# Moving scatters, key tiles, first maxima and row clears in a two-layer cross-attention and expert kernel

## The chip, the cores and the metric

The kernel runs on one core of a Trainium2 chip. The metric is the device time of one execution in microseconds (us). All data are 32-bit floats.

## The reference, cut to what matters

There are four batches of 512 rows of 256 numbers (`x`) and four contexts of 1601 rows. Two layers follow each other, and each is a cross-attention and then a mixture of experts:

```python
x = x + _L0_xattn_ref(ctx_1024, _layernorm(x), ...)   # 8 heads of 128, biases
x = x + _L0_ffn_ref(_layernorm(x), ...)               # 8 experts, top 2, capacity 512
x = x + _L1_xattn_ref(ctx_1024, _layernorm(x), ...)   # 8 heads of 32
x = x + _L1_ffn_ref(_layernorm(x), ...)               # 8 experts, top 2, no capacity
```

In the first expert layer each row goes to its two best experts. The rows of an expert are numbered in order of arrival, and each expert takes 512 of them:

```python
slot = jnp.where(valid, bin_ids * capacity + offsets, E * capacity)
xb = jnp.zeros((E * capacity + 1, hs), x.dtype).at[slot].set(xf[src])
h = jax.nn.gelu(jnp.einsum('ech,ehf->ecf', xb, w1))
y = jnp.einsum('ecf,efh->ech', h, w2).reshape(E * capacity, hs)
out = jnp.zeros((T, hs), x.dtype).at[src].add(flat_w[order][:, None] * yv)
```

The second attention is softmax(q k) v for each head, with keys and values projected from the raw context.

## The kernel before, in words

The kernel has four stages, one after the other.

Stage a, to 1609 us, is the first attention, batch after batch. While batch b is attended, the rows of batch b-1 are normalised, routed and scattered: `route` returns three steps. `normalize` is the layer norm, `choose` finds the two experts of every row and its slot, and `send` writes the rows with eight indirect DMAs from GpSimd's queue into a tensor in device memory, `slot_x` (L308). The scatters of one batch write the same tensor, so each waits for the one before. The last batch has no attention behind it, so its three steps lie in stage b.

Stage b is the first expert layer. Each expert's 512 slots are taken in two halves of 256: all eight experts run over half 0, then, after a branch, all eight over half 1. `all_experts` drives a half. For each expert `fetched` loads its rows from `slot_x` (sx, L1171) and its two weights (L1174, L1175), `turned` transposes the rows (L1183, L1184), `hidden` makes the hidden layer (L1193) with a Gelu (L1200), and `results` makes the output (L1207) and stores it into `slot_y` (L1216). Weights, rows and hidden tiles have two buffers. The first half holds only rows of the first three batches; the branch (L1282) reads whether that was so, and redoes the experts if not.

Beside the experts a generator does other work, two slices per expert: `keys_first` in half 0 (routing of the last batch, and the second attention's keys and values of batch 0, in 15 steps) and `keys_next` in half 1 (keys and values of batch 1, adding batch 0's expert outputs, batch 0's queries, and the score maxima of the attention's first unit). `collect` gathers expert outputs from `slot_y` with indirect DMAs on GpSimd's queue (L327); `add_collected` adds them to x on VectorE (L344).

A second generator, `clears`, writes constants into device memory with DMAs on SyncE's queue (SP), four per expert: the second halves of `slot_y` (eight of 256 KB), then `rows_a` and `rows_b` (41 of 530 KB, one of them half of that), which the last stage's scatters need in a cleared state. Their source is the tile `empty`. `tc.keep_in_program_order` holds a DMA behind what was written before it on its queue, and nothing more. Otherwise the order within a queue in this stage is drawn up by a scheduler that takes what is ready, earliest written first; so work can be drawn forward, across the branch too.

Stage c is the second attention, 16 units of (batch, group of four heads, half of the queries), each of 13 steps of one key tile. `maxima` makes the scores of a unit in seven pieces (L1109) and reduces them on VectorE (L1120). `negated` (L1129) and `to_row` (L1142, L1146) put the negated maxima into a row of the query tile `asked`. `weights` (L1357) multiplies `keyed`, which holds 32 key rows and a row of ones per head, with `asked`, and an Exp (L1370) makes the softmax weights. `add_weights` (L1379) sums them and `weigh` (L1388) multiplies them with the values. There are two `keyed` tiles, one for each group of heads; both are set to ones and zeros at the head of the stage (L1334, L1335) and filled by `load_keys` (L1341). The order of PE, VectorE, ScalarE and GpSimd is fixed as written in the steps. `put(step, f)` hangs work on a step; SP's order is left to the scheduler.

Stage d, from 2618 us, is the second expert layer. The pools `soon` and `turns` live from stage b to the end of stage c; the pools `b_...` and `c_...` live in their own stage, and a stage's pool takes over space of the stage before.

Of the kernel before, what the change touches and what calls it, by code (L numbers as in the profile page):

```python
# [8 lines left out]
F32 = mybir.dt.float32  # L9
I32 = mybir.dt.int32  # L10
AF = mybir.ActivationFunctionType
ALU = mybir.AluOpType
# [4 lines left out]
P = 128  # L17
B, S, D = 4, 512, 256
M = 1601
NT = S // P  # L20
NX = B * NT
DC = D // P
# [14 lines left out]
H1, DH1 = 8, 32  # L37
HG = P // DH1

E, FF = 8, 1024  # L40
# [4 lines left out]
CT = HALF // P  # L45
NOWHERE = 65536.0
# [11 lines left out]
PAY = D + 1 + E  # L58
# [12 lines left out]
def xattn_ffn_twice(ctx: ExitStack, tc: tile.TileContext, a: dict, out: bass.AP):  # L71
    nc = tc.nc
# [105 lines left out]
    slot_y = dram.tile([SLOTS, D], F32, name="slot_y")  # L178
# [160 lines left out]
    def add_collected(b, got, tiles=range(NT)):  # L339
        for t in tiles:  # L340
            for k in range(2):
                j = b * NT + t
                xs = x[b][:, t, :]
                nc.vector.scalar_tensor_tensor(  # L344
                    xs, got[2 * t + k], prob[k][:, j : j + 1], xs, ALU.mult, ALU.add
                )
# [31 lines left out]
        nc.sync.dma_start(rbias, a["br"].partition_broadcast(P))  # L378
        nc.sync.dma_start(b2, a["b2"])

    def clear_rows(empty):

        for rows in (rows_a, rows_b):
            n = rows.shape[0]
            for i in range(0, n, 4 * P):
                some = rows[i : min(i + 4 * P, n), :]

                tc.keep_in_program_order(
                    nc.sync.dma_start(
                        some.rearrange("(p r) d -> p r d", p=P),  # L390
                        empty.unsqueeze(1).to_broadcast([P, some.shape[0] // P, PAY]),
                    )
                )
                yield

    def route2(b, two, psum, tag, first=0, n=NT):

# [148 lines left out]
    with ExitStack() as st:  # L546
# [3 lines left out]
        rt = st.enter_context(tc.tile_pool(name="a_rt", bufs=1, side="right"))  # L550
        one = st.enter_context(tc.tile_pool(name="a_one", bufs=1))
# [333 lines left out]
        empty = scrap[:, 0, :]  # L885
# [14 lines left out]
        for n in range(n_steps + 4):  # L900
            b, h, t = n // (H0 * NT), n // NT % H0, n % NT
            if n < n_steps:
                if t == 0:
# [3 lines left out]
                    g = n // NT + 1  # L907
# [141 lines left out]
    for t in shift + asked:  # L1049
        nc.vector.memset(t, 0.0)  # L1050

    def queries(b, qT):
        xn = soon.tile([P, NT, D], F32, tag="xn", name="xn")
        mv = ln_moments(turns, x[b], NT)
        root = ln_root(turns, mv, NT)
        yield
        mv, rs = ln_scale(turns, mv, NT, root)
        for i in range(NT):
            ln_apply(xn, x[b], mv, rs, i)
        yield  # L1060
        xnT = soon.tile([P, DC, S], F32, tag="xnT", name="xnT")
        transposed(banks["s"], "s", xnT, xn, NT)
        yield
        for o in range(DC):
# [10 lines left out]
            yield  # L1075

    units = [(b, o, f) for b in range(B) for o in range(DC) for f in range(2)]
    qTs = {}

# [76 lines left out]
    with ExitStack() as st:  # L1156
# [8 lines left out]
        def slots(of, e, half):  # L1165
            s0 = e * CAP + half * HALF
            return of[s0 : s0 + HALF, :].rearrange("(t p) d -> p t d", p=P)

        def fetched(e, half):
            sx = two.tile([P, CT, D], F32, tag="sx", name="sx")  # L1170
            nc.sync.dma_start(sx, slots(slot_x, e, half))  # L1171
            w1 = two.tile([P, DC, FF], F32, tag="w1", name="w1")
            w2 = two.tile([P, FC, D], F32, tag="w2", name="w2")
            nc.sync.dma_start(w1, a["w1"][e].rearrange("(c p) f -> p c f", p=P))  # L1174
            nc.sync.dma_start(w2, a["w2"][e].rearrange("(c p) d -> p c d", p=P))  # L1175
            return e, half, sx, w1, w2

        def turned(e, half, sx, w1, w2):
            sxT = two.tile([P, DC, HALF], F32, tag="xT", name="sxT")
            tp = ps_t.tile([P, DC, CT, P], F32, tag="m", name="tp_x")  # L1180
            for c in range(DC):
                for t in range(CT):
                    nc.tensor.transpose(tp[:, c, t, :], sx[:, t, c * P : (c + 1) * P], ident)  # L1183
            nc.vector.tensor_copy(sxT, tp.rearrange("p c t q -> p c (t q)"))  # L1184
            return e, half, sxT, w1, w2
# [50 lines left out]
        empty = rt.tile([P, PAY], F32, name="empty")  # L1236
        nc.gpsimd.memset(empty, 0.0)
        nc.gpsimd.memset(empty[:, D : D + 1], NOWHERE)

        def clears():  # L1240

            for e in range(E):
                tc.keep_in_program_order(
                    nc.sync.dma_start(
                        slots(slot_y, e, 1), empty[:, :D].unsqueeze(1).to_broadcast([P, CT, D])
                    )
                )
                yield
            yield from clear_rows(empty)

        clear = clears()
        kvs = []

        def keys_first():
            normalize()
            yield
            choose()
            send()
            yield
            *kv, steps = keys_values(ps_s, "s", 0)  # L1260
            kvs.append(kv)
            for k, f in enumerate(steps):
                f()
                if k % 2:
                    yield

        normalize, choose, send = route(B - 1, rt, soon, ps_t, "m")
        all_experts(0, keys_first())
# [22 lines left out]
        def keys_next():  # L1291
            *kv, steps = keys_values(ps_s, "s", 1)
            kvs.append(kv)
            for f in steps[:6]:
                f()
            yield
# [12 lines left out]
            negated(0)  # L1309
            to_row(0)  # L1310

        all_experts(1, keys_next())
        assert next(clear, None) is None

# [5 lines left out]
    with ExitStack() as st:  # L1320
# [5 lines left out]
        ps_m = st.enter_context(tc.tile_pool(name="c_ps_m", bufs=1, space=PSUM))  # L1326
        banks.update(s=ps_s, m=ps_m)

        keyed = [one.tile([P, 2, M], F32, name=f"keyed{o}") for o in range(DC)]
        of_ones = ones[:, 0:1].to_broadcast([P, M])
        for t in keyed:
            nc.scalar.activation(t[:, 0], of_ones, AF.Copy, scale=in_row[:, 0:1])  # L1334
            nc.vector.tensor_scalar(t[:, 1], of_ones, in_row[:, 0:1], None, ALU.mult)  # L1335

        def load_keys(b, o):
            for pair in range(2):
                for s in range(2):
                    i = 2 * pair + s  # L1340
                    nc.sync.dma_start(  # L1341
                        keyed[o][64 * s : 64 * s + 32, pair, :],
                        kvs[b][0][o][i * DH1 : (i + 1) * DH1, :],
                    )


        by_pool = (1, 4, 7, 10)
# [121 lines left out]
        def put(step, *fs):  # L1469
            at.setdefault(step, []).extend(fs)  # L1470
# [9 lines left out]
        for b in range(B):  # L1480
# [20 lines left out]
            if 1 <= b and b + 1 < B:  # L1501
# [8 lines left out]

                spread(s0 + 2, projected(), 2, 16)
        put(per_batch * (B - 1) + 4, load_first_weights)

        load_keys(0, 0)
        load_keys(0, 1)
        ordered = st.enter_context(in_order(*computing))

        for g in range(3):
            maxima(1, g)
        ahead = {}  # L1520
        for u in range(1, n_units):
            for g in range(len(pieces)):
# [422 lines left out]
```

## Time and profile before

| what | value |
|---|---|
| median of three runs | 2953.87 us (2949.18 to 2956.38) |
| profiled execution | 2949.11 us |
| its span | 2947.0 us |
| PE busy | 2770.3 us (94%) |
| VectorE, ScalarE, GpSimd busy | 1466.2, 937.7, 392.5 us |
| mean granted TensorE clock | 0.973 |
| stage a, to 1590 us: PE busy | 1553.65 of 1590.0 us |
| stage b, 1590 to 1927 us: PE busy, DMA share | 308.70 of 337.0 us, 0.77 |
| stage c, 1927 to 2618 us: PE busy, DMA share | 602.62 of 691.0 us, 0.13 |
| stage d, 2618 to 2947 us: PE busy, DMA share | 305.29 of 329.0 us, 0.51 |

A line of busy time by stretch gives the stretch, its length, the busy time of each engine with its number of records, the granted clock (1.00 is full), the mean busy share of the 16 DMA engines, and GB/s. A matmul of this kernel shows as two records. A timeline line gives start, duration, engine, source line, operation, and in brackets the engine's idle time before it with what ended it. "SPq" is a queue's own instruction, such as the issue of a DMA.

### The profile page before, as it was taken

What the parts mean: (1) busy time and instruction counts of PE and PEld (TensorE: products, weight loads), DVE (VectorE), ACT (ScalarE), POOL (GpSimd) and SP (SyncE); (2) the same over time, 40 slices, a digit from 0 to 9 for tenths busy, and PEclk for the clock granted to TensorE, in tenths of its full rate; (3) what the DMA queues carried; (4) which work ended last, traced back from release to release, by engine and by line L of the source; (5) the groups of instructions that cost most, each with busy time, mean ns of one, the idle gap of its engine ahead of it and who ended that gap; (6) DMA issues with size and microseconds to landing.
All of it is one profiled execution on the core that took longest, in us unless ns stands there. A gap on an engine that the chain in (4) does not pass through costs nothing. (4 is left out here: it accounts for less than half of the span.)

```text
span 2947.0 us, 36216 instructions
## 1 busy us (share of the span) xinstructions
PE 2770.3 (94%) x13686; PEld 1883.4 (64%) x13686; DVE 1466.2 (50%) x2333; ACT 937.7 (32%) x1325; POOL 392.5 (13%) x301
## 2 busy tenths in 40 slices
PE   6999999999999999999999799988989898889997
PEld 2666667666766666666666587744444444467886
DVE  6445456544575544454444202267767768742110
ACT  3323334233342333332332112134434344331221
POOL 0000000100001000010000101021314233333442
PEclk9999999999999999999999899999999999999999
DMA  5444443343434333343346798610101021035663
GB/s 162 113 108 113 104 112 85 102 106 92 104 98 109 95 91 92 89 109 94 91 99 185 199 255 235 185 46 16 30 28 48 19 66 63 11 114 154 180 188 82
DMA packets 197448, 314.94 MB, mean 107 GB/s; under 512 B 44007, under 2 KB 118056, under 8 KB 194440
## 3 DMA queue, kind: packets, MB, share of 16 engines
q1 hardware_dynamic: 157512, 227.52, 29.1%
q0 software_dynamic: 15168, 49.23, 5.7%
q10 hardware_dynamic: 24576, 35.68, 4.7%
q8 instruction: 114, 1.87, 0.3%
q14 instruction: 78, 0.64, 0.1%
HBM read 114.64 MB, written 51.86 MB: 56 GB/s over the span
## 5 line engine op out<-in xcount | busy, mean ns | idle before, releaser
L806 DVE TENSOR_REDUCE top<-ps_s 128x1 f32<-128x2113 f32 x128 | 301.9, 2358 | 585.2 <-PE ps_s L798 585.2
L835 PE MATMUL ps_o<-pT,v 128*128 128x256 f32 x2176 | 521.1, 381 | 0.5 <-DVE inv L813 0.5
L798 PE MATMUL ps_s<-kT,qT 128*128 128x512 f32 (+1 forms) x1280 | 488.8, 526 | 6.5 <-ACT attn L812 6.4
L835 PEld LDWEIGHTS ps_o<-pT,v 128*128 128x128 f32 x2176 | 410.0, 191 | 114.5 <-issue 68.3
L812 ACT ACTIVATE attn<-ps_s,top 128x2113 f32<-128x2113 f32 x128 | 258.9, 2023 | 477.5 <-DVE top L806 433.2
L798 PEld LDWEIGHTS ps_s<-kT,qT 128*128 128x128 f32 x1280 | 241.8, 191 | 252.9 <-issue 236.5
L827 DVE STREAM_TRANSPOSE pT<-swapped 128x2176 f32<-128x2176 f32 x128 | 312.4, 2441 | 31.0 <-DMA swapped<-attn 20.4
L1120 DVE TENSOR_REDUCE tops<-ps_s 128x2 f32<-128x1024 f32 (+1 forms) x224 | 238.1, 1105 | 149.6 <-PE ps_s L1109 149.2
L747 PE MATMUL ps_k<-kvin,wkv 128*128 128x512 f32 (+1 forms) x640 | 263.8, 535 | 4.1 <-DVE mv_g L685 2.1
L1357 PE MATMUL ps_w<-asked,keyed 64*128 64x256 f32 (+1 forms) x1664 | 244.7, 416 | 21.1 <-DVE tops L1120 9.6
L781 PE MATMUL ps_v<-wkv,kvin 128*128 128x256 f32 x1088 | 254.6, 381 | 0.7 <-ACT v L788 0.6
L1357 PEld LDWEIGHTS ps_w<-asked,keyed 64*128 64x128 f32 (+1 forms) x1664 | 147.5, 190 | 146.6 <-ACT pT L1370 61.8
L1370 ACT ACTIVATE pT<-ps_w 128x1024 f32<-128x1024 f32 (+1 forms) x176 | 179.3, 1023 | 193.7 <-PE ps_w L1357 191.9
L781 PEld LDWEIGHTS ps_v<-wkv,kvin 128*128 128x128 f32 x1088 | 205.0, 190 | 35.9 <-ACT v L788 6.0
L1379 DVE TENSOR_TENSOR sum<-sum,pT 128x1024 f32<-128x1024 f32 (+1 forms) x128 | 183.2, 1431 | 10.4 <-ACT pT L1370 4.0
L760 ACT ACTIVATE kT<-ps_k,bqk 128x512 f32<-128x512 f32 (+1 forms) x160 | 96.8, 620 | 266.5 <-DMA swapped<-attn 129.0
L1379 POOL TENSOR_TENSOR sum<-sum,pT 128x1024 f32<-128x1024 f32 x48 | 122.6, 2554 | 347.5 <-ACT pT L1370 347.3
L747 PEld LDWEIGHTS ps_k<-kvin,wkv 128*128 128x128 f32 x640 | 116.4, 192 | 78.5 <-issue 67.4
L1109 PE MATMUL ps_s<-kv,qT 32*128 32x512 f32 (+1 forms) x1024 | 135.4, 574 | 14.6 <-ACT kv L1013 6.5
L788 ACT COPY v<-ps_v 128x512 f32<-128x512 f32 x144 | 79.7, 560 | 217.0 <-PE ps_v L781 150.2
L1193 PE MATMUL ps_h<-sxT,w 128*128 128x256 f32 x512 | 116.7, 386 | 2.9 <-ACT hT L1200 2.1
L1207 PE MATMUL ps_y<-w,hT 128*128 128x256 f32 x512 | 114.4, 380 | 0.2 <-DVE y L1215 0.2
(282 smaller groups left out, 2731.5 us busy)
## 6 DMA issues: line engine op xcount, KB each, us to landing
swapped<-attn SPq DMA_DIRECT2D x1536, 68.0 KB, 2.1
swapped<-attn ACTq DMA_DIRECT2D x512, 68.0 KB, 2.2
w<-in_w_dram SPq DMA_DIRECT2D x32, 1024.0 KB, 10.2
rows_b<-empty SPq DMA_DIRECT2D x36, 530.0 KB, 11.3
w_e<-in_wall_dram SPq DMA_DIRECT2D x4, 2052.0 KB, 9.3
cw<-in_ctxT_dram SPq DMA_DIRECT2D x4, 1601.0 KB, 12.5
keyed<-kv SPq DMA_DIRECT2D x32, 200.1 KB, 3.8
ctx_b<-in_ctx_dram SPq DMA_DIRECT2D x3, 1536.0 KB, 8.0
```

What stands on the lines that cost most here:

```text
L747: nc.tensor.matmul(ps[:, :n], lhsT=wkv[:, c, hs], rhs=kvin[:, c, : NB - 1, k, :] if k < 4 else kvin[:, c, NB - 1, :, :], start=c == 0, sto ...
L781: nc.tensor.matmul(ps[:, k, :], lhsT=flat_kvin[c][:, j * P : (j + 1) * P], rhs=wkv[:, c, cols], start=c == 0, stop=c == DC - 1,)
L798: nc.tensor.matmul(flat[:, j0 : j0 + n], lhsT=qT[:, t * P : (t + 1) * P], rhs=kT[:, j0 : j0 + n], start=True, stop=True,)
L806: nc.vector.tensor_reduce(top, flat[:, :L], AX.X, ALU.max, negate=True)
L812: nc.scalar.activation(attn[:, :L], flat[:, :L], AF.Exp, bias=top, accum_out=total)
L827: nc.vector.transpose(pT[:, :, k * P : (k + 1) * P].rearrange("p c (a i) -> p a c i", a=4), swapped.rearrange("p a (c i) -> p a c i", i=32),)
L835: nc.tensor.matmul(ps, lhsT=v[:, j - parts[part][0], (h % 2) * DH0 : (h % 2 + 1) * DH0], rhs=pT[:, j, :], start=j == 0, stop=j == NB - 1,)
L1109: nc.tensor.matmul(pss[i // 2][:, i % 2, at : at + n], lhsT=qTs[b][rows, o, q0 : q0 + P], rhs=kvs[b][0][o][rows, j0 : j0 + n], start=True, ...
L1120: nc.vector.tensor_reduce(tops[u][:, t : t + at // n, 2 * pair : 2 * pair + 2, j0 // 512], of, AX.X, ALU.max,)
L1357: nc.tensor.matmul(ps[:r, s, pair * QH : (pair + 1) * QH], lhsT=keyed[o][64 * s : 64 * s + 64, pair, j * P : j * P + r], rhs=asked[u % 3][ ...
L1370: nc.scalar.activation(pT[:r], ps[:r], AF.Exp)
L1379: (nc.gpsimd if k else nc.vector).tensor_tensor(to, to, pT[:r], ALU.add)
```

## The change

The change does six things:

1. `send()` of the last batch, written before between `choose` and the keys of batch 0, is written in the 21st slice of half 0, which lies after expert 7's rows are fetched.
2. `all_experts` gives the side work three slices per expert instead of two, and the key steps of half 0 come one per slice.
3. The first of the two key tiles moves into the pool `soon`. It is set in the 21st and loaded in the 22nd slice of half 0. The second stays in stage c; it is set in step 4 and loaded in step 8.
4. The first three maxima of unit 1, written before at the head of stage c, come after unit 0's in half 1, and `to_row(0)` comes after the first of them.
5. The row clears leave stage b. They are written one by one in steps 2 to 42 of stage c.
6. The clears of `slot_y` are written one per expert of half 0, and `empty` moves into `soon`.

```diff
-    def clear_rows(empty):
+    def clear_rows():
+        def clear(some):
+            tc.keep_in_program_order(
+                nc.sync.dma_start(
+                    some.rearrange("(p r) d -> p r d", p=P),
+                    empty.unsqueeze(1).to_broadcast([P, some.shape[0] // P, PAY]),
+                )
+            )
         for rows in (rows_a, rows_b):
             n = rows.shape[0]
             for i in range(0, n, 4 * P):
...
+                yield lambda some=rows[i : min(i + 4 * P, n), :]: clear(some)
...
+    keyed = [soon.tile([P, 2, M], F32, name="keyed0")]
...
+    def init_keys(t):
+        of_ones = ones[:, 0:1].to_broadcast([P, M])
+        nc.scalar.activation(t[:, 0], of_ones, AF.Copy, scale=in_row[:, 0:1])
+        nc.vector.tensor_scalar(t[:, 1], of_ones, in_row[:, 0:1], None, ALU.mult)
+    empty = soon.tile([P, PAY], F32, name="empty")
...
             for e in range(E):
                 done = hidden(*here)
                 next(beside, None)
-                for _ in range(4):
-                    next(clear, None)
+                if half == 0:
+                    clear_results(e)
                 if e + 1 < E:
                     here = turned(*fetched(e + 1, half))
+                next(beside, None)
                 if last:
                     results(*last)
                 next(beside, None)
...
             normalize()
             yield
             choose()
-            send()
             yield
             *kv, steps = keys_values(ps_s, "s", 0)
             kvs.append(kv)
-            for k, f in enumerate(steps):
+            for f in steps:
                 f()
-                if k % 2:
-                    yield
+                yield
+            for _ in range(len(steps) + 2, 3 * E - 4):
+                yield
+            send()
+            init_keys(keyed[0])
+            yield
+            load_keys(0, 0)
...
-            for f in steps[:6]:
-                f()
-            yield
-            add_collected(0, got0)
-            for k, f in enumerate(steps[6:]):
+            for k, f in enumerate(steps):
+                if k == 6:
+                    add_collected(0, got0)
                 f()
                 if k % 3 == 2:
                     yield
...
             negated(0)
-            to_row(0)
+            for g in range(3):
+                maxima(1, g)
+                yield
+                if g == 0:
+                    to_row(0)
...
-        keyed = [one.tile([P, 2, M], F32, name=f"keyed{o}") for o in range(DC)]
-        of_ones = ones[:, 0:1].to_broadcast([P, M])
-        for t in keyed:
-            nc.scalar.activation(t[:, 0], of_ones, AF.Copy, scale=in_row[:, 0:1])
-            nc.vector.tensor_scalar(t[:, 1], of_ones, in_row[:, 0:1], None, ALU.mult)
...
+        keyed.append(one.tile([P, 2, M], F32, name="keyed1"))
...
-        load_keys(0, 0)
-        load_keys(0, 1)
+        for k, f in enumerate(clear_rows()):
+            put(2 + k, f)
+        put(4, lambda: init_keys(keyed[1]))
+        put(8, lambda: load_keys(0, 1))
         ordered = st.enter_context(in_order(*computing))
-        for g in range(3):
-            maxima(1, g)
```

More of the change, by code (lines that the diff above doesn't have):

```diff
@@ L385, in clear_rows @@
             for i in range(0, n, 4 * P):
[L386 to L393, printed above, removed]
-                yield
+                yield lambda some=rows[i : min(i + 4 * P, n), :]: clear(some)
     def route2(b, two, psum, tag, first=0, n=NT):
@@ L1050, in xattn_ffn_twice, with load_keys @@
         nc.vector.memset(t, 0.0)
+    keyed = [soon.tile([P, 2, M], F32, name="keyed0")]
+    def load_keys(b, o):
+        for pair in range(2):
+            for s in range(2):
+                i = 2 * pair + s
+                nc.sync.dma_start(
+                    keyed[o][64 * s : 64 * s + 32, pair, :],
+                    kvs[b][0][o][i * DH1 : (i + 1) * DH1, :],
+                )
+    def init_keys(t):
[3 more added lines that the diff above has]
+    empty = soon.tile([P, PAY], F32, name="empty")
+    nc.gpsimd.memset(empty, 0.0)
+    nc.gpsimd.memset(empty[:, D : D + 1], NOWHERE)
     def queries(b, qT):
@@ L1075, in queries @@
             yield
+    kvs = []
     units = [(b, o, f) for b in range(B) for o in range(DC) for f in range(2)]
@@ L1234, in all_experts, with clear_results @@
             assert next(beside, None) is None
[L1236 to L1246, printed above, removed]
-                )
-                yield
-            yield from clear_rows(empty)
-        clear = clears()
-        kvs = []
+        def clear_results(e):
+            tc.keep_in_program_order(
+                nc.sync.dma_start(
+                    slots(slot_y, e, 1), empty[:, :D].unsqueeze(1).to_broadcast([P, CT, D])
+                )
+            )
         def keys_first():
@@ L1261, in keys_first @@
             kvs.append(kv)
-            for k, f in enumerate(steps):
+            for f in steps:
                 f()
-                if k % 2:
-                    yield
+                yield
[5 more added lines that the diff above has]
+            load_keys(0, 0)
         normalize, choose, send = route(B - 1, rt, soon, ps_t, "m")
@@ L1293, in keys_next @@
             kvs.append(kv)
-            for f in steps[:6]:
-                f()
-            yield
-            add_collected(0, got0)
-            for k, f in enumerate(steps[6:]):
+            for k, f in enumerate(steps):
+                if k == 6:
+                    add_collected(0, got0)
                 f()
@@ L1309, in keys_next @@
             negated(0)
-            to_row(0)
+            for g in range(3):
[3 more added lines that the diff above has]
+                    to_row(0)
         all_experts(1, keys_next())
-        assert next(clear, None) is None
     with ExitStack() as st:
@@ L1327, in xattn_ffn_twice @@
         banks.update(s=ps_s, m=ps_m)
-        keyed = [one.tile([P, 2, M], F32, name=f"keyed{o}") for o in range(DC)]
-        of_ones = ones[:, 0:1].to_broadcast([P, M])
-        for t in keyed:
-            nc.scalar.activation(t[:, 0], of_ones, AF.Copy, scale=in_row[:, 0:1])
[L1335 to L1344, printed above, removed]
+        keyed.append(one.tile([P, 2, M], F32, name="keyed1"))
         by_pool = (1, 4, 7, 10)
```

## The prediction

> **What bounds the kernel now.** I began with the slices of the page: PE is at 9 almost everywhere, with a 7 in the 23rd (1621 to 1695 us) and 8s from the 27th on (1915 us). As the change touches only the expert stage and the head of the attention, I next took busy time by stretch there, cut where the waits lie.
>
> ```profile
> core 0: us, PE busy (x) PEld busy (x) DVE busy (x) ACT busy (x) POOL busy (x), PEclk, DMA share, GB/s
> 1590.00:1657.20 67.20, 65.94 (x294) 51.33 (x292) 27.90 (x87) 15.04 (x24) 4.95 (x6) 1.00 0.81 238
> 1657.20:1677.90 20.70, 0.03 (x2) 0.01 (x1) 0.23 (x1) 1.54 (x2) 5.87 (x6) 0.59 0.27 74
> 1677.90:1690.00 12.10, 11.32 (x42) 9.27 (x43) 0.87 (x2) 2.08 (x4) 0.00 (x0) 0.72 0.94 278
> 1690.00:1769.00 79.00, 79.00 (x375) 69.05 (x374) 7.21 (x14) 12.25 (x21) 0.00 (x0) 1.00 1.01 251
> ...
> 1800.00:1926.70 126.70, 126.52 (x610) 101.87 (x610) 26.50 (x33) 19.85 (x35) 0.00 (x0) 1.00 0.66 184
> ```
>
> The reader is to see that PE is full in every stretch of this stage but the second, which is empty, and that the clock is 0.59 there and 0.72 after it. In 1690 to 1769 the DMA engines are full too (1.01), yet PE waits for none of it: the row clears ride along for nothing.
>
> The waits of PE, and those of SP's queue, give the empty stretch one cause; the timeline gives its course.
>
> ```profile
> PE tp_x L1183 <- DMA sx<-slot_x: 20.7, 1, 20.7
> ...
> SPq L1171 <- DMA slot_x<-xn,slot: 23.2, 1, 23.2
> ```
>
> ```profile
> 1638.07 0.99 POOL L308 DMA_INDIRECT slot_x<-xn,slot  x1 [15.03 <-ACT kv L112]
> 1649.64 0.98 POOL L308 DMA_INDIRECT slot_x<-xn,slot  x1 [10.58 <-DMA slot_x<-xn,slot]
> ...
> 1672.74 0.98 POOL L308 DMA_INDIRECT slot_x<-xn,slot  x1 [1.55 <-DMA slot_x<-xn,slot]
> 1675.12 0.89 SPq L1171 DMA_DIRECT2D sx<-slot_x  x2
> ...
> 1677.89 1.12 PE L1183 MATMUL tp_x<-ident,sx 128*128 128x128 f32 x4 [20.67 <-DMA sx<-slot_x]
> 1679.04 0.69 DVE L1184 COPY sxT<-tp_x 128x512 f32<-128x512 f32 x1 [21.56 <-PE tp_x L1183]
> 1679.79 6.11 PE L1193 MATMUL ps_h<-sxT,w 128*128 128x256 f32 x16 [0.78 <-DVE sxT L1184]
> ```
>
> Eight scatters go one at a time: each waits for the one before to land (11.6 us while the DMA engines are full, 2.6 us at the end). Expert 2's rows are read from the same tensor, so their load stands behind the eighth scatter. Everything else on PE, batch 0's keys included, has been drawn forward and is used up at 1657.2.
>
> Second place, the chain of waits where experts end and attention begins:
>
> ```profile
> 1927.81 2.14 DMA slot_y<-y
> 1930.36 0.88 issue
> 1931.23 1.05 DVE keyed L1335
> 1932.28 1.15 DVE tops L1120
> 1933.47 4.34 PE ps_s L1109 x12
> 1937.81 2.06 PE ps_w L1357 x8
> 1939.93 1.28 ACT L1370
> 1941.23 1.03 ACT sum L1370
> ```
>
> Experts end at 1927.0, and the first Exp starts at 1941.2: 14.2 us in which the output store has to land, the key tiles are set, and unit 1's maxima stand ahead of the first weights.
>
> **What the Trainium skill says.** "TensorE: Matmul & The Clock Gate", What's actually happening: PE's clock halves after an idle window of about 3.4 us and comes back after about as long at work. The trace agrees: 16 ps_h records take 6.11 us after the stall, 3.62 us otherwise. "DMA: Bandwidth & Descriptors", Anatomy of one DMA — SWDGE (gpsimd) path: about 2 us of a DMA are fixed, mostly the receipt of its last write. The trace's chained scatters at 2.6 us agree. The same page, Issuing engines are not separate DMA queues: DMAs of every engine share the same 16 engines. The 11.6 us of the second scatter, issued beside four clears, agrees.
>
> **Part by part.** *Scatters.* They are now written after expert 7's first-half load, and as writes to a tensor still being read they can't be drawn ahead of it. Expert 2's load then depends only on scatters of older batches, done by 1330 us. Gone: 20.7 us of waiting, 0.8 us for the copy after it, 2.5 us of slow ps_h and 0.5 us of slow tp_x: **24.5 us**. PE's next limit is its own work: 14.3 us an expert, beside which 2.5 MB an expert need 10 us at the 251 GB/s seen. What is late next is the scatters themselves. Expert 7's load is issued at 1711.7, the halves' last results end at 1769.0 and the next half's load goes at 1775.7: cover of 64 us less about 3 us of landing, so 61 us for eight, or 7.6 us each. The eight took 37 us in all before, the first two in the worst load; without clears the DMA share falls by about half, and batch 2's eight, at a share of 0.41 around 1315 us, were issued 2.7 to 3.8 us apart; I take 3 to 6 us each, 24 to 48 us. Cost 0, bounds 0 and 29 us (second rival). POOL has the gathers of batch 0 behind them; they start at the branch anyway.
>
> *Row clears.* 41 DMAs, 22 MB, leave the experts and go to SP's queue in attention steps 2 to 42. No PE time was lost to them, so none comes back, except at the start of half 1: four clears there hold SP for 11.2 us, and the gather on the chain takes 6.3 us to land. Of 5.4 us idle in 1769 to 1800, 3.3 are the branch's; I take **1 us**, bounds 0 and 2. In the attention 22 MB at 251 GB/s are 88 us; DMA share there is 0.1. Queued near them on SP: the query loads (written 12 steps ahead, 34 us at 2.8 us a step) and the second key load (steps 8 to 26, about 50 us); on POOL's queue the gathers, added 13 steps after issue. A clear's landing of 11.3 us fits each slack. Cost 0, bounds 0 and 5. SP draws ready DMAs ahead of their step, as it does now with the query loads (asked<-qT x8 at 1861, the last at 1870), so some seven clears will land among the last experts: 3.8 MB, 15 us, against a weight lead of 21 us (one and a half experts). That too costs 0.
>
> *Result clears.* Eight as before, one per expert. The zero row moves to a pool that opens only when the first attention has ended (SP's cw load waits there for x L856 until 1612), so the first goes at 1612 instead of 1593; results are read after the branch only. If SP stood at it, expert 1's weights behind it would come some 17 us late, of which expert 0's results on PE cover 7: cost 0, bounds 0 and 10.
>
> *Keys and maxima.* Three maxima of unit 1 go beside the half-1 experts: 3 x 1.07 us on PE, which is full there, so +3.2 us before the experts' end, and the row of unit 0 (0.6 us) with them; DVE's 6 reduces (6.9 us) lie under PE (DVE is busy 26 of 127 us). keyed0 is set and loaded in half 0. At the boundary remain y's copy and its store landing (1930.3, 3.3 us after the experts' end), since the attention's tiles lie where y was; ps_w (1.1 us) and the table load (1.28 us) fit in that, or 1.3 us stick out. Before 14.2 us, after 3.2 + 0.6 + 3.3 to 4.6: a gain of 5.8 to 7.1, I take **6.5 us**. keyed1 is set in step 4: DVE 1.05 us and ACT 1.62 us, written in order; DVE has no gap from 1955 to 1967, so I charge **1.3 us**, bounds 0 and 2.7. keyed0's ACT 1.62 us before a Gelu may hold PE once: **0.3 us**.
>
> *Three slots of side work per expert instead of two* reorder PE's work, not its sum. I charge **1 us** for PSUM turns of closely placed maxima (bounds -1 and 3).
>
> Sum: -24.5 - 1 - 6.5 + 1.3 + 0.3 + 1 = **-29.4 us**. The profiled execution took 2949.1 us (span 2947.0 and 2.1 around it); the sum gives 2919.7 for it. It was as fast as the fastest of the three runs, whose median is 2953.87; for a median I predict **2924 us**.
>
> **Rivals.** *Boundary gain lost*: the first Exp waits for something else (the table load, DVE's backlog of 1955 to 1967, a store behind clears), so only the stall is gained: -22 us, 2932. For it: DVE is the limit soon after. Against: 9 us of DVE work leave that place.
>
> *The stall moves to the half boundary*: under weights alone each scatter still takes the 11.6 us of the worst case; 93 us against 61 leave 32, some 3 of it filled by batch 1's keys: 29 us lost of 29, about 2953. For it: the first three took 11.6, 8.2 and 4.6 us. Against: clears were in the queue then. From 7.6 us per scatter PE waits.
>
> *Slower: the clears stand ahead of loads that the attention needs.* At the 2.8 us that SP took per clear at its worst (11.16 us for four), 41 are 114 us. If all of them stood ahead of the second key load, needed 26 steps or 75 us in, unit 2 would start 39 us late: 2963. It starts to wait from 27 clears ahead and ends slower from 38. For it: SP draws ready DMAs forward. Against: each clear is held behind what is already written on SP, and only seven are written before that load.
>
> *The change doesn't do what it says*: if the load stayed behind the scatters, only the boundary would gain: 2947. A read can't need a later write, so I hold this unlikely.
>
> **How the numbers follow.** Forecast 0.66 (2916 to 2933); boundary lost 0.15 (2930 to 2943); stall moved 0.08; not done 0.04; slower 0.07. A measurement of this kernel tells about 0.3%, 9 us, from no change, so faster means below 2945. Faster 0.83 (the first two and a rest), same 0.10 (the stall moved, or not done), slower 0.07. The range, 2912 to 2944, holds the forecast with its unknown costs and nearly all of the second case.
>
> **What would show it.** Right: no wait of tp_x for sx over 3 us; scatters between about 1685 and 1740 with the last landed before the branch; first half's results ending near 1744; the first Exp within 5 us of the last expert; clears spread on SP from the last experts to about 2030 and no wait of PE, DVE or ACT on keyed, asked or g. Wrong: a wait of SP's sx load on slot_x after the branch; a wait of ps_w on keyed; new PE gaps in the first half by DVE or ACT.

## The result and the profile after

Six runs of the changed kernel had a median of 2926.10 us (2920.64 to 2930.95), six of the kernel before, run beside it, 2953.22 us. The ratio is 0.9909, with a 95% interval of 0.9894 to 0.9923: 27 us faster. The profiled execution took 2930.95 us, the slowest of the six; its span is 2929.2 us.

Busy time by stretch, after. The first three cuts are those shown of before; the fourth ends with half 0's last result, the fifth with half 1's.

```profile
core 0: us, PE busy (x) PEld busy (x) DVE busy (x) ACT busy (x) POOL busy (x), PEclk, DMA share, GB/s
1590.00:1657.20 67.20, 66.39 (x311) 54.16 (x310) 30.09 (x88) 16.74 (x25) 3.39 (x6) 1.00 0.59 195
1657.20:1677.90 20.70, 20.70 (x99) 18.22 (x98) 2.08 (x3) 4.16 (x7) 0.00 (x0) 1.00 0.55 171
1677.90:1690.00 12.10, 12.10 (x56) 9.70 (x55) 1.11 (x2) 2.38 (x4) 0.99 (x1) 1.00 0.50 174
1690.00:1746.10 56.10, 56.10 (x259) 47.66 (x259) 5.44 (x12) 7.75 (x13) 6.85 (x7) 1.00 0.44 143
1746.10:1919.10 173.00, 161.89 (x735) 124.75 (x733) 45.26 (x72) 28.80 (x48) 8.18 (x8) 0.97 0.74 203
```

The second stretch, which held 0.03 us of work, is now full. PE is full to the end of half 0, and the DMA share there is 0.44 where it was 1.01. The last line is the surprise: half 1 takes 173 us with 11 us of idle PE.

Waits of PE from 1590 to 1922 us (total, times, longest): sx has left the list, and smaller waits stand in its place.

```profile
PE ps_h L1218 <- ACT hT L1225: 4.2, 2, 3.9
PE ps_k L1008 <- PEq L1304: 3.3, 1, 3.3
PE ps_s L1134 <- DVE tops L1145: 1.8, 3, 0.7
PE ps_w L1365 <- DVE y L1240: 0.8, 1, 0.8
PE ps_y L1232 <- DVE y L1240: 0.8, 1, 0.8
PE ps_h L1218 <- DMA w<-in_w_dram: 0.7, 1, 0.7
```

The timeline of GpSimd: the scatters lie beside half 0, 2.5 to 7.1 us apart, and the first gather behind the branch finds them long done.

```profile
1688.46 0.99 POOL L308 DMA_INDIRECT slot_x<-xn,slot  x1 [61.88 <-DMA sx<-slot_x]
1691.51 0.98 POOL L308 DMA_INDIRECT slot_x<-xn,slot  x1 [2.06 <-DMA slot_x<-xn,slot]
...
1717.01 0.98 POOL L308 DMA_INDIRECT slot_x<-xn,slot  x1 [6.07 <-DMA slot_x<-xn,slot]
1719.53 0.98 POOL L308 DMA_INDIRECT slot_x<-xn,slot  x1 [1.54 <-DMA slot_x<-xn,slot]
1750.53 1.05 POOL L327 DMA_INDIRECT g<-slot_y,slot  x1 [30.02 <-DVEq L1304]
```

The timeline at the boundary to the attention:

```profile
1917.84 1.24 PE L1232 MATMUL ps_y<-w,hT 128*128 128x256 f32 x5
1919.12 0.69 DVE L1240 COPY y<-ps_y 128x512 f32<-128x512 f32 x1 [7.27 <-PE ps_y L1232]
1919.86 1.13 PE L1365 MATMUL ps_w<-asked,keyed 64*128 64x256 f32 x8 [0.79 <-DVE y L1240]
1922.32 1.28 ACT L1378 ACT_TABLE_LOAD   x1 [17.47 <-PE ps_s L1134]
1923.61 2.03 ACT L1378 ACTIVATE sum<-ps_w 128x1024 f32<-128x1024 f32 x2
```

Experts end at 1919.08, and the first Exp starts 4.5 us later. PE's ps_w waits for y's copy alone (0.79 us), but it isn't what the Exp waits for last. ScalarE's sequencer, the part that issues its instructions, holds the table load until the store of the last y has landed: the store is issued at 1919.84 and lands at 1921.95, and the sequencer, waiting on that store's semaphore since 1904.26, goes on at 1921.98. (The timeline names ps_s, which ended at about the same time; in "spaced, clears later" the table load starts at 1911.06, after the store's landing at 1910.90 and before ps_s ends at 1911.16.) So y's copy, the landing of its store and the table load of 1.28 us make up the 4.5 us. Before, the key tiles and unit 1's maxima came on top.

A table by stretch, for all kernels run, carries the rest. *Half 0* goes from the start of stage a's last record of x (L856, now L858) to the end of half 0's last ps_y, *half 1* from there to the end of the last ps_y, the *boundary* from there to the first Exp, the *attention* from there to the last `got`. The ratio is to the kernel before, run beside it. The stretches of a row come from one profiled execution, the median from four to twenty. Executions of one kernel differ by some us in a stretch, as the two rows of before and of changed show, and the profile of "clears later" is the slowest of its four, 8 us above their median.

| kernel | half 0 | half 1 | boundary | attention | median us | ratio [95%] |
|---|---|---|---|---|---|---|
| before | 157.8 | 158.0 | 14.2 | 665.4 | 2953.22 | 1 |
| before, again | 160.7 | 163.3 | 14.2 | 665.7 | 2960.84 | 1.0000 [0.9992, 1.0007] |
| changed | 132.2 | 172.9 | 4.5 | 665.2 | 2926.10 | 0.9909 [0.9894, 0.9923] |
| changed, again | 132.9 | 172.2 | 4.5 | 659.8 | 2924.25 | 0.9903 [0.9886, 0.9920] |
| scatters late alone | 140.4 | 167.5 | 14.2 | 667.3 | 2940.56 | 0.9944 [0.9930, 0.9957] |
| scatters early again | 149.7 | 179.0 | 4.5 | 661.7 | 2945.53 | 0.9963 [0.9949, 0.9977] |
| clears back | 149.9 | 171.7 | 4.3 | 659.7 | 2936.92 | 0.9940 [0.9925, 0.9956] |
| edge back | 131.4 | 180.4 | 12.9 | 665.1 | 2945.09 | 0.9972 [0.9963, 0.9982] |
| edge back, clears later | 131.1 | 167.2 | 12.9 | 664.1 | 2928.01 | 0.9898 [0.9883, 0.9914] |
| maxima back | 132.2 | 176.3 | 9.2 | 660.8 | 2930.93 | 0.9922 [0.9905, 0.9938] |
| maxima back, clears later | 132.6 | 166.1 | 9.2 | 663.4 | 2923.20 | 0.9888 [0.9872, 0.9904] |
| clears later | 132.7 | 173.3 | 4.3 | 664.2 | 2922.87 | 0.9889 [0.9873, 0.9904] |
| spaced | 132.8 | 168.0 | 4.5 | 659.9 | 2921.91 | 0.9894 [0.9876, 0.9912] |
| spaced, clears later | 132.2 | 163.1 | 4.4 | 658.4 | 2916.10 | 0.9864 [0.9849, 0.9879] |

### The profile page after: what moved, and what is told of

Read it like the earlier page. It is cut to its first block, busy times and chain, and to the rows that moved or that the text cites. A ratio compares the mean times of both kernels' runs of the same rounds, so it can differ in the third digit from the quotient of the medians.

```text
span 2929.2 us, 36226 instructions
## 1 busy us (share of the span) xinstructions
PE 2773.5 (95%) x13686; PEld 1883.9 (64%) x13686; DVE 1464.3 (50%) x2333; ACT 936.2 (32%) x1324; POOL 393.4 (13%) x301
```

## The experiments

**The two kernels again.** The changed kernel, unchanged:

> The changed kernel itself, for a second profile and as the measure of the three beside it. Theory: stall of the scatters gone (half 0 about 25 us shorter), boundary 10 us shorter, half 1 about 9 to 15 us longer; the wait of 3.9 us for a Gelu at the start of half 1 hangs on when the gathers land and will differ between executions. Expected 27 us (0.9909) below the kernel before. Rival: all that was seen in the first profile belongs to the change, so half 1 is again 173 us and the time 18 to 20 us below.

It came out at 0.9903, so the gain stands; half 1 is again 172 us, as the rival had it. The kernel before, for a second profile of it:

> The kernel before, unchanged, for a second profile of it. The changed kernel's own two profiles differ by 5.4 us in the attention (665.2 and 659.8 us from the first Exp to the last unit's output); the one profile of before has 665.4. Theory (the attention takes one of two courses by chance, in either kernel): 659 to 667 us here, and half 0, half 1 and the boundary as in the first profile within 1 us (157.8, 158.0, 14.2). Rival (the changed order at the attention's head makes the shorter course likelier, and before always takes the longer one): 665 to 667 us, and 2952 to 2956 in all.

The attention took 665.7 us, which fits either expectation and settles nothing between them. "Half 1 as in the first profile within 1 us" failed: it took 163.3 us instead of 158.0. Its list of waits has the reason:

```profile
PE tp_x L1183 <- DMA sx<-slot_x: 22.0, 2, 21.6
PE ps_h L1193 <- ACT hT L1200: 6.0, 2, 5.7
```

ps_h's wait for the first Gelu is 5.7 us here and was 1.8 us in the profile that the prediction rested on. That is 4 of the 5 us. The stall is nearly the same in both (21.6 and 20.7 us).

**Scatters late alone.** The kernel before, with `send()` alone moved:

```diff
             choose()
-            send()
             yield
...
+            for _ in range(5):
+                yield
+            send()
```

> The kernel before, with the eight scatters of the last batch alone written later (behind expert 7's first-half load); clears, keys and maxima stay where they were before. Theory (the stall is gained by the scatters' place alone): half 0 takes 132 to 134 us from stage a's end instead of 158, half 1 and the boundary stay at 158 and 14 us; about 24 us faster than before, 2930. Rival (beside the clears, with the DMA engines full, each scatter takes up to 11.6 us, so eight take 93 us against a cover of 61): tp_x waits for sx some 30 us at the start of half 1, and the time stays at 2953 or rises.

0.9944: 16 us, two thirds of what the theory gave. Half 0 is 8 us longer than in the changed kernel. PE lost that to a late weight load, which SP issued at 1725.15 behind five clears (8.44 us), and to the slow matmuls behind the wait:

```profile
1742.43 9.24 PE L1207 MATMUL ps_y<-w,hT 128*128 128x256 f32 x32 [5.43 <-DMA w<-in_w_dram]
```

GpSimd's timeline shows the rival's slow scatters too, if at 6.2 to 10.9 us each instead of 11.6:

```profile
1695.92 0.99 POOL L308 DMA_INDIRECT slot_x<-xn,slot  x1 [72.86 <-ACT hT L1200]
1704.88 0.98 POOL L308 DMA_INDIRECT slot_x<-xn,slot  x1 [7.97 <-DMA slot_x<-xn,slot]
1715.79 0.98 POOL L308 DMA_INDIRECT slot_x<-xn,slot  x1 [9.93 <-DMA slot_x<-xn,slot]
...
1759.87 0.98 POOL L308 DMA_INDIRECT slot_x<-xn,slot  x1 [8.66 <-DMA slot_x<-xn,slot]
1763.43 1.05 POOL L327 DMA_INDIRECT g<-slot_y,slot  x1 [2.58 <-SPq L1285]
```

The eight take 64 us, and PE's wait at the branch, which ends after the last is issued, is 6.4 us instead of 3.3. The rival's wait of tp_x for sx did not come. By stretch:

```profile
1660.00:1690.00 30.00, 30.00 (x133) 23.92 (x132) 3.88 (x6) 5.35 (x9) 0.00 (x0) 1.00 1.04 211
1690.00:1751.70 61.70, 56.27 (x257) 48.67 (x256) 4.75 (x11) 7.17 (x12) 6.87 (x7) 0.94 1.08 258
```

The DMA share is 1.04 to 1.08: with the stall gone the clears have to fit into 140 us, and the DMA engines are full.

**Scatters early again.** The changed kernel with `send()` back behind `choose()`:

> The changed kernel, with the scatters alone written early again, directly after the choice of experts. Theory (the clears' absence does not shorten the chain of eight landings by much): the wait of tp_x for sx comes back with 18 to 21 us, 22 to 25 us slower than the changed kernel, 2947 to 2949. Rival (without the clears in the DMA queues the first three scatters land in 3 to 4 us instead of 11.6, 8.2 and 4.6): the chain takes 28 us instead of 37, the wait is 9 to 12 us, and the time 2934 to 2938.

0.9963, which is 0.0054 to 0.0060, or 16 to 18 us, above the changed kernel's two ratios: between the two expectations. The scatters ran from 1638.25 to the loads at 1668.51, 30 us instead of 37, so in the kernel before the clears had lengthened the chain, and with it the stall; tp_x waited 6.0 us for sx, but the keys waited another 7.0 us for a context load issued only at 1656.30, and half 1 lost 6.1 us to a late w. Neither expectation foresaw that the loss would be split.

**Clears back.** The changed kernel with the row clears beside the experts:

```diff
+                if half or e > 1:
+                    for _ in range(4):
+                        next(rows_clear, lambda: None)()
...
-        for k, f in enumerate(clear_rows()):
-            put(2 + k, f)
```

> The changed kernel, with the row clears written beside the experts again, four per expert from expert 2 of half 0 to the end of half 1; scatters, keys and maxima stay as changed. Theory (the clears rode free in the kernel before only because the stall left the DMA engines idle; with the stall gone they fill the engines and stretch the scatters to 7 to 11 us each, as in the run with the scatters alone moved): half 0 of about 140 us instead of 132, the last scatter issued after the branch, half 1 of 170 to 175 us, and 2931 to 2935, 7 to 10 us slower than the changed kernel. Rival (what the prediction said: moving the clears is worth 1 us): half 0 of 132 to 134 us and 2923 to 2926.

0.9940, where the changed kernel had 0.9903 and 0.9909: about 10 us slower. Half 0 is 149.9 us, more than the theory's 140; the rival's 132 to 134 is out. The size is near the theory's, the way is another. The scatters were stretched, to 6.5 to 12.2 us apart, but the last was issued at 1759.88, before half 0 ended at 1762.21, and PE's wait at the branch is 3.1 us, no longer than in the changed kernel. What PE waited for is the load of the next context (batch 1's keys):

```profile
1721.72 9.33 SPq L387 DMA_DIRECT2D rows_b<-empty  x5
1731.09 2.40 SPq L999 DMA_DIRECT2D cw<-in_ctxT_dram  x1
1748.86 2.07 PE L1008 MATMUL ps_k<-cw 128*128 128x512 f32 x2 [12.18 <-DMA cw<-in_ctxT_dram]
```

SP issued it at 1731.09, behind clears; in the changed kernel, whose half 0 begins 1.6 us later, SP issued it at 1702.92, and PE does not wait for it. So here the clears cost PE time through a load that stands behind them on SP's queue and lands beside them, not through the scatters.

**Edge back.** The changed kernel with both key tiles set and loaded at the attention's head, and unit 1's maxima there too, as before:

```diff
-            init_keys(keyed[0])
-            load_keys(0, 0)
...
+        load_keys(0, 0)
+        load_keys(0, 1)
+        for g in range(3):
+            maxima(1, g)
```

> The changed kernel with both key tiles set and loaded at the head of the attention and the three maxima there too: only the scatters, the three slices and the clears remain of the change. Theory: the boundary is 14 us again (10 more), half 1 about 9 us shorter: expected 26 to 28 us below before, so the two edits of the boundary together are worth nothing as they were made. Rival: they are worth the 6.5 us that the prediction gave them: 20 us below before.

0.9972, a gain of only 8.6 us: none of the expectations had it so small, and the boundary (12.9 us) explains 8.4 us of the loss only. The rest is in half 1, 180.4 us. The timeline of SP and PE there:

```profile
1879.22 1.15 SPq L1199 DMA_DIRECT2D w<-in_w_dram  x1
1880.41 12.37 SPq L387 DMA_DIRECT2D rows_b<-empty  x5
1892.88 2.10 SPq L1200 DMA_DIRECT2D w<-in_w_dram  x1
```

```profile
1892.85 9.79 PE L1218 MATMUL ps_h<-sxT,w 128*128 128x256 f32 x32 [5.53 <-DMA w<-in_w_dram]
1908.42 8.84 PE L1232 MATMUL ps_y<-w,hT 128*128 128x256 f32 x32 [5.78 <-DMA w<-in_w_dram]
```

25 of the attention's 41 row clears have been drawn forward into half 1. Five of them hold SP for 12.37 us, and the second of the late weights is issued behind them. The first, issued at 1879.22 behind four others, lands beside the five, and PE starts on it 13.6 us after its issue. PE waits twice, 11.3 us, and the groups behind the waits take 9.79 and 8.84 us where 32 such records take 7.2; the granted clock was 0.50 from 1891.38 to 1898.21 and from 1905.04 to 1911.87. To test that, the clears were put where they can't be drawn forward, behind a query load that waits for the attention:

```diff
-            put(2 + k, f)
+            put(28 + k // 2, f)
```

> The run in which both key tiles and unit 1's maxima stood at the head of the attention again, now with the row clears written two a step from step 28 of the attention, behind a query load that cannot be drawn forward, so that none can land among the experts. Theory (that run lost its time to clears drawn ahead of the last experts' weights: 11.3 us of waits for w and 4.3 us of slow matmuls behind them): no wait for w over 1 us, half 1 back from 180 to about 165 us, 2929 to 2931. Rival (the edits at the boundary themselves are worth 20 us, and the waits for w only filled time that was lost anyway): 2943 to 2946.

0.9898: the theory held (2928.01, a little under its range), and the rival is out. No wait for w is left, and half 1 is 13.2 us shorter. It also gives the net worth of the edits at the boundary, against the changed kernel with the same late clears (0.9889, below): the boundary is 8.6 us shorter with them, half 1 6.1 us longer. The net, 0.0009 or some 3 us, is less than the intervals of the two ratios.

**Maxima back.** The changed kernel with unit 1's three maxima alone at the attention's head, first with the clears as changed, then with the clears later:

> The changed kernel with the first three maxima of unit 1 at the head of the attention again, and the row of unit 0 made directly after its maxima; all else as changed. Theory: half 1 is shorter by 3.2 us of matmuls and by the 5 to 6 us of crowding, the boundary longer by 4 to 5 us (three maxima with DVE's reduces before the second Exp): expected 31 us below before, 4 below the changed kernel. Rival: moving the maxima is a gain of its own, the time goes up to 22 us below before.

> Unit 1's three maxima stand at the head of the attention again, the first key tile stays early, and the row clears are written two a step from step 28 of the attention, so that none lands among the experts. Theory (moved and crowded, the maxima cost half 1 about as much, 3.4 us of matmuls and 5 us of waits and slow turns, as the 4.7 us by which the boundary is shorter and the rest of the attention's head): no wait for w, half 1 of about 166 us, boundary 9.2 us, 2920 to 2923, 0 to 4 us faster than the changed kernel and 4 to 6 slower than the version with the maxima spaced and the clears late. Rival (the maxima's move is worth 7 us, as the run with early clears said): 2929 to 2931.

With early clears it lost about 6 us to the changed kernel (0.9922), with late ones nothing that can be seen (0.9888 against 0.9889 for the changed kernel with late clears). Half 1 went from 176.3 to 166.1 us, and the wait for w, 7.3 us, vanished. So the first run's lesson, that the move of the maxima is worth 7 us, was false: it had measured the late weights. Moved as in the change, the maxima shorten the boundary by 4.9 us (9.2 to 4.3) and lengthen half 1 by 7.2 (166.1 to 173.3).

**Spaced, and clears later.** In half 1 the third slice of side work goes only to experts 0 to 3, so that from expert 4 on one maximum stands between any two groups of expert matmuls:

```diff
-                next(beside, None)
+                if half == 0 or e < 4:
+                    next(beside, None)
```

> The changed kernel, but half 1 has the third slice of side work only for its first four experts, so that two maxima never stand next to each other on PE and the last of them lies between the last two outputs. Theory: crowded maxima cost half 1 some 5 to 6 us (PE waits for the reduce of the one before), and 0.8 us more for the copy between the last two outputs: expected 31 to 33 us below before, 5 below the changed kernel, half 1 some 6 us shorter. Rival: the waits are only shifted, the time is the changed kernel's, 27 us below.

> The changed kernel, with the row clears alone written two a step from step 28 of the attention. Theory (of the changed kernel's loss in half 1, the clears drawn forward cost 0.9 us of wait for w, 0.4 for sx and about 1 us of slow matmuls; the crowded maxima cost the rest): 2 to 3 us faster than the changed kernel, 2921 to 2923, half 1 of 169 to 170 us with the waits for tops still there. Rival (the whole distance between the changed kernel and the version with maxima spaced and clears late is the clears'): 2916 to 2918.

> The run with the maxima spaced out (no third slice of side work with experts 4 to 7 of half 1), and with the row clears written two a step from step 28 of the attention, so that none lands among the experts. Theory (the 20 clears drawn forward cost that run 2.6 us of waits for w and 1 to 2 us of slow matmuls, and the clears cost nothing in the attention): no wait for w, 2 to 4 us faster than that run, 2918 to 2920. Rival (clears pressed into fewer steps stand ahead of the key and query loads of the attention): a wait of ps_w on keyed or asked, 2924 or more.

Spacing alone gave 2921.91 us, 31.8 below before but only 2.3 below the changed kernel beside it, though half 1 is 4.2 us shorter; 2.6 us of waits for w remain in it. Clears later alone gave 2922.87, in the theory's range; but half 1, expected at 169 to 170 us, stayed at 173.3, no shorter than the changed kernel's. Both together gave 2916.10 us, 0.9864 [0.9849, 0.9879], the best version: half 1 fell to 163.1. The two losses lay in part over each other. In the second run of the changed kernel and in "maxima back", both with early clears, the late weights come at nearly the same time (the first line is of the one, the second of the other):

```profile
1895.26 7.14 PE L1218 MATMUL ps_h<-sxT,w 128*128 128x256 f32 x32 [0.90 <-DMA w<-in_w_dram]
1895.92 9.10 PE L1218 MATMUL ps_h<-sxT,w 128*128 128x256 f32 x32 [7.26 <-DMA w<-in_w_dram]
```

Without the three maxima PE waits 7.26 us for them, with the maxima 0.90: the crowded maxima fill time in which the weights are late anyway. In the "spaced" run the weights came earlier (1892.68), so a part of the gain shows there. In the totals each removal alone is worth some 2 to 6 us and both some 11 to 13; the intervals are too wide to tell more from the totals, so that the two cover each other rests on the waits.

What crowding is shows in PE's timeline, first in the changed kernel, then in the spaced one with late clears:

```profile
1845.08 1.14 PE L1134 MATMUL ps_s<-kv,qT 32*128 32x512 f32 x8
1846.15 0.66 PE L1208 MATMUL tp_x<-ident,sx 128*128 128x128 f32 x4
1847.53 2.26 PE L1134 MATMUL ps_s<-kv,qT 32*128 32x512 f32 x8 [0.73 <-DVE tops L1145]
```

```profile
1849.96 1.14 PE L1134 MATMUL ps_s<-kv,qT 32*128 32x512 f32 x8
1851.04 7.17 PE L1218 MATMUL ps_h<-sxT,w 128*128 128x256 f32 x32
1858.14 1.14 PE L1134 MATMUL ps_s<-kv,qT 32*128 32x512 f32 x8
```

Two maxima with only a transpose between them make the second wait 0.73 us for VectorE's reduces (2.36 us a pair) to free its tiles in PSUM, the memory into which PE writes. It then takes 2.26 us instead of 1.14, as its second half starts only when the second reduce has ended. With 7 us of expert matmuls between them each takes 1.14 and waits for nothing. By groups, ps_s takes 14.2 us in "clears later" and 11.2 in "spaced, clears later", with 1.8 and 0.0 us of waits, for the same 88 records.

## Why the prediction was right, and where it was not

The total was right: 2926.1 against 2924, within the range. Its steps were not all.

*Scatters, -24.5 us*: right. Half 0 fell by 25.6 us and its results end at 1746.1 (1744 was expected), no tp_x waits for sx, and the scatters lie between 1688 and 1722, 2.5 to 7.1 us apart where 3 to 6 were expected.

*Row clears, "1 us, bounds 0 and 2"*: the first step that failed. "No PE time was lost to them, so none comes back" judged the clears by PE's waits in the kernel before, where the stall hid their cost. There they had lengthened the chain of scatters (37 us, and 30 without them). With the stall gone they delay loads: a weight by 5.4 us in "scatters late alone", a context by 12.2 in "clears back". Scatters late without the clears' move gain 16 us, and the changed kernel with its clears back keeps 18 of its 27 to 29, so that their move is worth some 10 us, not 1. The rival of the stall moved to the half boundary did not come true in any run: even with the clears in the queues, and scatters 6.2 to 12.2 us apart, tp_x waits for sx there by no more than 0.7 us. (The 11.6 us that the prediction gives the second scatter lie between the first two issues, so they are the first one's landing.)

*"Some seven clears will land among the last experts"*: 20 did, from 1825 us on, and 25 in "edge back". The prediction took it that only the seven written before the second key load can go ahead of it; SP issued 20 before that load (1935.01). Why the scheduler let them pass stays open. The step said that it costs 0 against a weight lead of 21 us. The changed kernel itself waited only 0.7 us for w, but because crowded maxima held PE up beside it. The mechanism is the slower rival's, clears ahead of loads, at another place: not the attention's key loads but the experts' last weights, and it took 11.3 us of waits in "edge back".

*"1 us for PSUM turns of closely placed maxima, bounds -1 and 3"*: mis-sized. Between "clears later" and "spaced, clears later", which differ in the spacing alone, half 1 differs by 10.2 us; 4.8 us of that are ps_s's own (3.0 because its records overlap less, 1.8 in waits), and 0.8 the wait for y's copy between the last two results, which a maximum covers when spaced. Up to 3.4 more go with the clock, which was at 0.50 for 13.7 us of half 1 in the one and 6.8 in the other; whether crowding caused that is not shown. The moved maxima are not the whole of it: without them, but with three slices an expert, half 1 still takes 166.1 and 167.2 us ("maxima back" and "edge back" with late clears) where before takes 158.0 and 163.3, and PE waits there 1.4 us for the reduces of unit 0's maxima.

*Half boundary, -1 us*: not seen. ps_h's wait for the first Gelu was 1.8 and 5.7 us before, 3.9 and 2.7 after.

*Boundary, -6.5 us*: right for the boundary, in its parts too. It predicted 3.3 to 4.6 us from the experts' end to the first Exp, made of y's copy, its store's landing and, if it sticks out, the table load; measured 4.5, with the store landed after 2.9 and the table load behind it. From 14.2 that is 9.7 us, less the 3.8 us of work moved into half 1: 5.9. But half 1 paid 6.1 us for these edits and not 3.8, so that as the change made them their net worth is some 3 us, within the noise. The table splits the boundary: 12.9 us with the key tiles and maxima at the head, 9.2 with the first key tile early, 4.3 to 4.5 with the maxima early too.

*keyed1, keyed0, clears in the attention*: PE waits for none of keyed, asked and g between 1920 and 2590 us of after. "Clears later" puts all 41 into the attention, at a DMA share of 0.43 from 1924 to 2265 us where the changed kernel has 0.26, and is not slower. Cost 0 was right.

So half 1, predicted at +3.8 us (3.2 + 0.6 + 1 - 1), came out at +15 between the two profiles shown, +12 between the means of both profiles of each kernel. By these means half 0 is 26.7 us shorter (24.2 predicted), the boundary 9.7 (10.3), the attention 3.1 (1.3 longer predicted). Half 1 cost 8 us more than was foreseen, half 0 and the attention together 7 less: that these misses nearly cancel is luck, and the total is nearer to the forecast than the steps are. The two profiles first shown, whose executions lay 4 us under and 5 us over their medians, differ by 18 us only.

The attention took 665.2 or 659.8 us in the changed kernel, 665.4 and 665.7 in the kernel before. The five profiles with key tiles and maxima at the attention's head have 664.1 us or more, the nine others 658.4 to 665.2. That leans towards a part of the gain, some 4 us between the means, lying there. But the clock differs as well: in the changed kernel's two profiles it was at 0.50 for 82.3 and 59.5 us of the attention, and over all 14 profiles a longer attention goes with more such time (a correlation of 0.84). How much of the 4 us is the change's own stays open.

## What to carry to other kernels

Transfers that cost nothing that shows beside a stall may cost when the stall goes: price their cover again after the edit that removes it. A DMA that nothing waits for is still in somebody's queue; pin it behind something that can't run early, or the scheduler will put it ahead of loads on which the next matmul waits. Two losses that cover each other show only a part of their size when one is removed, so run both removals together before calling either worthless.

## What the runs showed of the hardware that was not expected

An issue isn't free for the queue that makes it. The prediction had read four clears that hold SP for 11.16 us in the kernel before, and counted them at the half boundary and in one rival. With the DMA share at 1.09 (1825 to 1900 us of "edge back"), SP stood 12.37 us at five clears of 530 KB, 2.5 us each. The Trainium skill, "DMA: Bandwidth & Descriptors", Issuing engines are not separate DMA queues, calls the time on the sequencer usually small relative to the DMA itself; here it is not small. By an estimate from this trace, moving the five at the 263 GB/s of those 12.37 us takes 10 us, nearly as long as SP stood.

A chained scatter takes longer when the DMA engines are fuller: the eight are 2.5 to 7.1 us apart at a DMA share of 0.59 (1688.46 to 1722 us of the changed kernel), 6.2 to 10.9 us at 1.08 (1695.92 to 1759.87 us of "scatters late alone").

The same wait has different aftermaths. Behind the wait for the first Gelu, eight ps_h records took 1.99 us after 3.2 us of idleness in "edge back" and 3.47 us after 2.9 in the same kernel with late clears. The Trainium skill, "TensorE: Matmul & The Clock Gate", What's actually happening, says that the window in which activity is judged runs freely, so that the point of the change depends on where in it the work falls. The two records agree with that: the clock was 0.50 from 1768.99 to 1772.40 in the second, and full in the same time of the first. So do the traces as a whole: in the 14 profiles all 596 stretches between two changes of the clock last a multiple of 3.41 us. The attention's lengths may differ for the same reason; they go with the time at 0.50, but no run here shows what sets that.
